# Comparison rows kept in a PSUM bank, and running counts of bins by a comparison and an addition in one VectorE operation

## The chip, the cores and the metric

The kernel runs on one core of a Trainium2 chip. The metric is the device time of one execution in microseconds (us). The core's engines are TensorE (PE in the profile, its weight loads PEld), VectorE (DVE), ScalarE (ACT), GpSimd (POOL) and SyncE (SP), which here only issues transfers. SBUF and PSUM are its memories of 128 partitions; PSUM has eight banks of 512 float32 values per partition, and matrix products are written there.

## The reference

A graph layer with 12,500 nodes of 128 features and 400,000 edges, sorted by `dst`. Cut to what is computed:

```python
h    = maximum(layernorm(x), 0) @ W_in2f.T               # 12500 x 128
Wij  = (smu(edge_attr_20 @ W_f1.T + b_f1) @ W_f2.T + b_f2) * edge_weight[:, None]
x_ij = h[dst] * Wij                                      # 400000 x 128
agg  = segment_sum(x_ij, src, num_segments=12500)
out  = x + smu(agg @ W_o1.T + b_o1) @ W_o2.T + b_o2
# smu(v) = ((1 + a) * v + (1 - a) * v * erf(mu * (1 - a) * v)) / 2, a = 0.01, mu = 2.5
```

`dst` is sorted, so the rows `h[dst]` of neighbouring edges lie close together. `src` is random, so the sum over `src` needs a sort.

## The kernel before

**Tiles.** 128 edges make a tile (3125 of them), four tiles a *group* (782; `GRP`), two groups a *super* (`SUP` tiles), and 59 supers (118 groups) an *epoch*; the seventh and last epoch has 37 supers (74 groups, the last one a single tile). Nodes are cut into 98 *bins* of 128 (`NB`); the bin of an edge is the upper part of `src` (`hi_b`), its place in the bin the lower part (`lo_b`).

**A group's way.** Its 512 edges run through PE as `pu` (line 478, first layer), GELU on ACT (`ge`, 486), `sm` on DVE (494), `pw` on PE (528). `ph` (509) picks the rows of h by a one-hot matrix `oh` (made once per super at line 386); ACT copies it to `hg` (517); DVE multiplies the two to `mt` (538). PE transposes `mt` to `pt` (548), ACT scales it by the edge's weight into the message buffer `ms` (558; six buffers), DVE writes the edge's `lo` as a 129th column (555), and POOL scatters the four tiles, 128 rows each, into a DRAM buffer of the epoch by four indirect transfers (561). An `ms` buffer is free again once its transfers have landed.

**Where a row goes.** Each bin has a region of `CAP` rows in the epoch's buffer (768 rows, 512 in the last epoch), and an edge takes the next free slot. `bins` (392 to 415) makes, per group, the one-hot `po` over bins (399: 128 partitions x 4 tiles x 98 bins) by comparing a row of bin numbers `irow_b` with `hi_b`, and the running count `co` of each partition over the tiles before (410 and 413: one addition of 98 float16 values per tile, each on the result of the one before). `count` (419 to 445) multiplies `co` by ones and `po` by a triangle with 32768 on its diagonal into the PSUM tile `pc` (426, 427; two banks in turn), so that the edge's own bin holds 32768 plus its slot; `read` (447) takes that out on ACT by a Relu with a sum (456), and `number` (459) makes the row index `ix` of slot and bin on DVE (465).

**Summing up.** While epoch k scatters, the rows of epoch k-1 are read back bin by bin (`fetch`, 575), 12 x 128 rows at a time. `choose` (586) makes their one-hot matrices `se` by comparing the row 0..127 in `irow` with the column of `lo` values (593: 128 x 1536 float32), and `add` (597) multiplies rows and `se` into `pg` (606) and adds that to `agg` (617, 619). This starts four groups into an epoch (`WAIT`) and is spread over the rest of it. The last epoch's sums, and the output layers (`half`, 320, and `rest`, 332), come after the last scatter. In the first epoch the other rows of h are made instead (`others`, 660: lines 178 to 212).

**Order.** Around all this the order on PE, DVE, ACT and SP is the program's own (`manual_schedule`). Within the loop over groups (678) a step does `turn` and `send` of group g, `number`, `weigh`, `gather`, `take` of g+1, half of the sums, `mix` of g+1, `hide`, `bend`, `count`, `read`, `smooth` of g+2, `bins` of g+3 and the other half of the sums. So DVE's order in a step is `ms` (555), `ix`, `mt`, `sm`, `oh` in every second step, `po`, the `co` chain, and `se` and `agg` wherever the sums call for them. POOL holds nothing but the scatters once the loop runs. Before the loop the same functions are called for groups 0 to 2 (lines 633 to 654).

PSUM is full: `pc` and `pg` have two banks each, `ph`, `pu`, `pw` and `pt` one.

Of the kernel before, what the change touches and what calls it, by code (L numbers as in the profile page):

```python
# [9 lines left out]
F32 = mybir.dt.float32  # L10
BF = mybir.dt.bfloat16
# [3 lines left out]
ALU = mybir.AluOpType  # L15
# [4 lines left out]
P = 128  # L20
# [9 lines left out]
GRP = 4  # L30
# [9 lines left out]
def gnn_kernel(  # L40
# [19 lines left out]
    nc = tc.nc  # L60
# [4 lines left out]
    NB = (N + P - 1) // P  # L65
    LASTB = N - (NB - 1) * P
    def chunks(total, step):
        return [(a, min(step, total - a)) for a in range(0, total, step)]
# [7 lines left out]
    for n in PARTS:  # L76
        n = min(n, left)
# [6 lines left out]
    CAP, ZMIN = [], []  # L84
    for a, n in eps_of:
# [9 lines left out]
    const = ctx.enter_context(tc.tile_pool(name="const", bufs=1))  # L95
# [17 lines left out]
    irow = const.tile([P, P], F32, name="irow")  # L113
    nc.gpsimd.iota(irow, pattern=[[1, P]], base=0, channel_multiplier=0,
                   allow_small_or_imprecise_dtypes=True)
    irow_b = const.tile([P, P], BF, name="irow_b")
    nc.vector.tensor_copy(irow_b, irow)

    tri = const.tile([P, P], F16, name="tri")
    lift = const.tile([P, P], F32, name="lift")  # L120
# [97 lines left out]
    with tc.tile_pool(name="prep", bufs=1) as prep, \  # L218
# [44 lines left out]
        for a, m in chunks(NT // P, GRP) + [(NT // P, 0)]:  # L263
# [8 lines left out]
            elif NT % P:  # L272
                m = NT % P
# [71 lines left out]
    with tc.tile_pool(name="ld", bufs=4) as ld, \  # L345
# [4 lines left out]
            tc.tile_pool(name="ps2", bufs=2, space=PSUM) as ps2, \  # L350
            tc.tile_pool(name="ps1", bufs=1, space=PSUM) as ps1, \
            tc.manual_schedule(engines={ET.PE, ET.DVE, ET.Activation, ET.SP}):
        NF = 4
        fbufs = []
        for i in range(NF):
            fb = ld.tile([P, SUP * P], F32, name=f"f{i}", bufs=1)
            nc.vector.memset(fb, 1.0)
            fbufs.append(fb)
        groups = [(t0 + a, g) for t0, nt in sups for a, g in chunks(nt, GRP)]
        NG = len(groups)  # L360
        PER = SUP // GRP
        epoch = [k for k, (a, n) in enumerate(eps_of) for _ in range(n)]
        first = {a * PER: k for k, (a, n) in enumerate(eps_of)}
        loaded, onehot, bins_of, slots, hidden, taken = {}, {}, {}, {}, {}, {}

        def load(s):
# [3 lines left out]
            e0, n = t0 * P, nt * P  # L370
            fb = fbufs[s % NF]
            nc.sync.dma_start(fb[0:R, :n], f_t[:, e0:e0 + n])
# [16 lines left out]
        last = {}  # L389
        begins = {}  # L390

        def bins(g):


            if g >= NG:
                return
            t, n = groups[g]
            po = cnt.tile([P, GRP, NB], F16, name="po")
            nc.vector.tensor_tensor(po[:, :n], irow_b[:, :NB].unsqueeze(1).to_broadcast([P, n, NB]),  # L399
                                    hi_b[:, t:t + n].unsqueeze(2).to_broadcast([P, n, NB]), op=ALU.is_equal)  # L400
            co = cnt.tile([P, GRP + 1, NB], F16, name="co")
            if g in first:
                k = first[g]
                nc.vector.memset(co[:, 0], 0.0)
                m = sum(groups[i][1] for i in range(g, min(g + eps_of[k][1] * PER, NG)))
                begins[k] = (t, cnt.tile([P, max(n for _, n in eps_of) * SUP], F32, name="hic", bufs=2))
                nc.vector.tensor_scalar(begins[k][1][:, :m], hi_b[:, t:t + m], float(CAP[k]), None, op0=ALU.mult)
            else:
                pl, cl, nl = last.pop(0)
                nc.vector.tensor_add(co[:, 0], cl[:, nl - 1], pl[:, nl - 1])  # L410
            more = g + 1 in first or g + 1 in (NG, BY)
            for j in range(1, n + more):
                nc.vector.tensor_add(co[:, j], co[:, j - 1], po[:, j - 1])  # L413
            last[0] = (po, co, n)
            bins_of[g] = (po, co)

        counts = {}
# [1 line left out]
        def count(g):  # L419

            if g >= NG:
                return
            n = groups[g][1]
            po, co = bins_of.pop(g)
            pc = ps2.tile([P, GRP, NB], F32, name="pc")
            nc.tensor.matmul(pc[:, :n], ones_h, co[:, :n], start=True, stop=False)  # L426
            nc.tensor.matmul(pc[:, :n], tri, po[:, :n], start=False, stop=True)  # L427
            counts[g] = pc
            if g + 1 == BY:
                pt = ps1.tile([P, GRP * P], F32, name="ph")[:, :NB]  # L430
                nc.tensor.matmul(pt, ones_h, co[:, n], start=True, stop=True)
                mm = cnt.tile([P, 2], F32, name="mm")
                nc.vector.tensor_reduce(mm[:, 0:1], pt[:, :NB - 1], op=ALU.max, axis=AX.X)
                nc.vector.tensor_scalar(bad[:, 3:4], mm[:, 0:1], float(ZMIN[0]), None, op0=ALU.is_gt)
            if g + 1 in first or g + 1 == NG:

                k = epoch[g // PER]
                pt = ps1.tile([P, GRP, P], F32, name="ph")[:, 0, :NB]
                nc.tensor.matmul(pt, ones_h, co[:, n], start=True, stop=True)
                mm = cnt.tile([P, 2], F32, name="mm")  # L440
                nc.vector.tensor_reduce(mm[:, 0:1], pt, op=ALU.max, axis=AX.X)
                nc.vector.tensor_reduce(mm[:, 1:2], pt[:, :NB - 1], op=ALU.min, axis=AX.X)
                i = 4 + 2 * k
                nc.vector.tensor_scalar(bad[:, i:i + 1], mm[:, 0:1], float(CAP[k]), None, op0=ALU.is_gt)
                nc.vector.tensor_scalar(bad[:, i + 1:i + 2], mm[:, 1:2], float(ZMIN[k]), None, op0=ALU.is_lt)
# [140 lines left out]
        def choose(k, c):  # L586

            b = c * SPAN[k]
            if b >= NB:
                return  # L590
            m = min(SPAN[k], NB - b) * Q[k]
            se = rowp.tile([P, ROWS, P], F32, name="se", bufs=2)
            nc.vector.tensor_tensor(se[:, :m], irow.unsqueeze(1).to_broadcast([P, m, P]),  # L593
                                    rows_in[c][:, :m, P:P + 1].to_broadcast([P, m, P]), op=ALU.is_equal)
            sel[c] = se

        def add(k, b, q):

            g = b % GRP
            c, i = b // SPAN[k], b % SPAN[k]  # L600
            if q == 0 and g == 0:
                pgs[0] = ps2.tile([P, GRP, P], F32, name="pg")
            if q == 0 and i == 0:
                choose(k, c + 1)
            o = i * Q[k] + q
            nc.tensor.matmul(pgs[0][:, g, :], rows_in[c][:, o, 0:P], sel[c][:, o, :], start=(q == 0),  # L606
                             stop=(q == Q[k] - 1))
            if q < Q[k] - 1:
                return
            if i == SPAN[k] - 1 or b == NB - 1:  # L610
                rows_in.pop(c), sel.pop(c)
                fetch(k, c + AHEAD)
            if g == GRP - 1 or b == NB - 1:
                dst = agg[:, (b - g) * P:(b + 1) * P]
                src = pgs[0][:, :g + 1].rearrange("p b n -> p (b n)")
                if k == 0:
                    nc.vector.tensor_copy(dst, src)
                else:
                    nc.vector.tensor_add(dst, dst, src)
# [18 lines left out]
        for g in range(3):  # L638
            bins(g)
        count(0)  # L640
        read(0)
        count(1)
        read(1)
        number(0)
# [33 lines left out]
        for g in range(NG):  # L678
            s = g // PER
            k = epoch[s]  # L680
# [22 lines left out]
            if k and i == WAIT - 2:  # L703
                choose(k - 1, 0)
# [14 lines left out]
            hide(g + 2)  # L719
            bend(g + 2)  # L720
            count(g + 2)
            read(g + 2)
            smooth(g + 2)
            if g % PER == 0:
                pick((g + 4) // PER)
            bins(g + 3)
            parts(k - 1, hi)
            step()
            assert k == 0 or next(h_steps, None) is None
        k = EPOCHS - 1  # L730
        begin(k)
        choose(k, 0)
        mids, ends = [], []
        units_in = {}
# [41 lines left out]
    with tc.If(flag > 0):  # L776
        with tc.tile_pool(name="gl", bufs=1) as gl, tc.tile_pool(name="gps", bufs=1, space=PSUM) as gps:
# [11 lines left out]
            with tc.For_i(0, NT, 1) as t:  # L789
# [26 lines left out]
                                               op1=ALU.mult, accum_out=dup)  # L816
# [87 lines left out]
```

## Time and profile before

| | |
|---|---|
| median of three runs | 4601.06 us (4593.67 to 4603.17) |
| the profiled execution | 4605.67 us, its span 4603.9 us |
| granted TensorE clock, mean | 0.949 |
| PE busy | 3824.8 us (83%) |
| POOL busy | 3355.9 us (73%) |
| DVE busy | 3181.2 us (69%) |
| ACT busy | 2809.9 us (61%) |
| first scatter's start, last one's start | 93.6 us, 4405.8 us |
| DMA | 808.84 MB, mean 176 GB/s |

A row of the list of groups reads: line, engine, operation, result<-operands, shapes, count, then the engine's busy time with them in us, the mean of one in ns, and behind the second bar the engine's idle time just before them with what ended most of it. A row of a line's own view has the durations as minimum/median/maximum in ns, and the first and last start in us. A row of the timeline has the start in us from the span's start, the duration in us, engine, line and operation, and in brackets the idle time before it with what ended it.

### The profile page before, as it was taken

The numbers are of one execution on the slowest core, as the hardware profiler recorded it, in microseconds if no ns is written. First come the engines' busy times: TensorE is split into PE (matmuls) and PEld (weight loads), VectorE is DVE, ScalarE is ACT, GpSimd is POOL, SyncE is SP. The second block draws the span as 40 slices with busy tenths as digits, with TensorE's granted clock in tenths as the row PEclk, the third lists the DMA queues.
The fourth block names the chain that finished last, engine by engine and source line by source line (L and its number), as shares of the span: only waits on it lengthen the run. The fifth ranks groups of instructions, "written<-read, shape, count | busy, mean of one in ns | idle before, by whom it ended". The sixth has DMA issues, their size and how long they took to land. (4 is left out here: it accounts for less than half of the span.)

```text
span 4603.9 us, 73307 instructions
## 1 busy us (share of the span) xinstructions
PE 3824.8 (83%) x18332; PEld 2340.7 (51%) x18596; DVE 3181.2 (69%) x8458; ACT 2809.9 (61%) x11054; POOL 3355.9 (73%) x3137
## 2 busy tenths in 40 slices
PE   4777787988879888879888878888798888799967
PEld 2334434555545555545555545555455555466656
DVE  5876676767667667757766767667576676687746
ACT  3776785666656666657666666666576666566500
POOL 1777777777777777777777777777777777777720
PEclk9999998999999999989999989999999999899978
DMA  6945565656646656646655556556465555466556
GB/s 187 212 139 169 157 167 173 193 174 184 181 131 214 190 175 183 181 145 206 190 180 172 168 171 199 172 179 186 125 209 173 169 172 166 138 197 183 164 179 175
DMA packets 457331, 808.84 MB, mean 176 GB/s; under 512 B 82228, under 2 KB 258630, under 8 KB 456512
## 3 DMA queue, kind: packets, MB, share of 16 engines
q1 hardware_dynamic: 328136, 573.65, 43.1%
q0 software_dynamic: 101504, 212.48, 14.2%
q10 hardware_dynamic: 27256, 17.94, 1.3%
q8 instruction: 147, 2.41, 0.2%
q14 instruction: 288, 2.36, 0.2%
HBM read 449.68 MB, written 354.07 MB: 175 GB/s over the span
## 5 line engine op out<-in xcount | busy, mean ns | idle before, releaser
L561 POOL DMA_INDIRECT buf<-ms,ix x3125 | 3349.1, 1072 | 1050.3 <-issue 268.7
L558 ACT ACTIVATE ms<-pt,w_sb 128x128 f32<-128x128 f32 x3125 | 903.2, 386 | 905.8 <-DMA buf<-ms,ix 699.8
L606 PEld LDWEIGHTS pg<-se,rw 128*128 128x128 f32 x7840 | 1087.1, 195 | 189.9 <-issue 51.7
L606 PE MATMUL pg<-se,rw 128*128 128x128 f32 x7840 | 1109.0, 278 | 35.7 <-DVE se L593 35.6
L456 ACT ACTIVATE jk<-pc,nbig 128x98 f32<-128x98 f32 x3125 | 1034.8, 361 | 12.3 <-PE pc L427 11.9
L548 PE MATMUL pt<-ident,mt 128*128 128x128 f32 x3125 | 512.8, 288 | 561.3 <-DVE mt L538 558.1
L528 PE MATMUL pw<-sm,w_f 128*128 128x512 f32 x1564 | 923.5, 674 | 27.1 <-DVE sm L494 21.6
L538 DVE SCALAR_TENSOR_TENSOR mt<-pw,b,hg 128x512 f32<-128x512 f32 x782 | 584.7, 748 | 514.6 <-ACT hg L517 511.3
L478 PE MATMUL pu<-f,w_f 128*128 128x512 f32 x1564 | 813.8, 602 | 2.6 <-DVE sm L494 2.5
L486 ACT ACTIVATE ge<-pu 128x512 f32<-128x512 f32 x782 | 472.9, 605 | 395.4 <-PE pu L478 360.2
L593 DVE TENSOR_TENSOR se<-irow,rw 128x1536 f32<-128x1536 f32 x327 | 572.6, 1751 | 193.0 <-DMA rw<-buf 159.5
L456 ACT ACTIVATION_READ_ACCUMULATOR jk<-pc,nbig 128x1 f32 x3125 | 705.0, 226 | 0.0
L548 PEld LDWEIGHTS pt<-ident,mt 128*128 128x128 f32 x3125 | 355.3, 145 | 668.5 <-DVE mt L538 664.1
L509 PE MATMUL ph<-oh,hw 128*128 128x512 bf16 (+1 forms) x2082 | 651.5, 396 | 16.1 <-issue 3.1
L494 DVE SCALAR_TENSOR_TENSOR sm<-pu,ge 128x512 f32<-128x512 f32 x782 | 535.6, 685 | 150.6 <-ACT ge L486 143.8
L517 ACT ACTIVATE hg<-ph 128x512 f32<-128x512 f32 x782 | 471.4, 603 | 210.2 <-PE ph L509 207.9
L413 DVE TENSOR_TENSOR co<-co,po 128x98 f16<-128x98 f16 x2351 | 503.7, 214 | 81.3
L509 PEld LDWEIGHTS <-hw 128*128 128x128 bf16 x2346 | 239.2, 102 | 585.9 <-issue 493.6
L399 DVE TENSOR_TENSOR po<-irow_b,hi_b 128x392 f16<-128x392 bf16 x782 | 436.8, 559 | 0.0
L555 DVE CAST ms<-lo_b 128x4 f32<-128x4 bf16 x782 | 150.6, 193 | 315.9 <-DMA buf<-ms,ix 312.8
L528 PEld LDWEIGHTS pw<-sm,w_f 128*128 128x128 f32 x1564 | 244.1, 196 | 165.7 <-DVE sm L494 163.1
L426 PE MATMUL pc<-co,ones_h 128*128 128x392 f16 x782 | 257.9, 330 | 13.3 <-DMA rbc<-rel_dram 12.8
(114 smaller groups left out, 1771.2 us busy)
## 6 DMA issues: line engine op xcount, KB each, us to landing
rw<-buf SPq DMA_DIRECT2D x326, 774.0 KB
buf<-zero SPq DMA_DIRECT2D x294, 387.0 KB
rbc<-rel_dram SPq DMA_DIRECT2D x390, 256.0 KB
buf<-ms,ix POOLq DMA_INDIRECT x3125
hw<-h_dram SPq DMA_DIRECT2D x391, 96.0 KB
f<-in_f_t SPq DMA_DIRECT2D x390, 80.0 KB
buf<-zero SPq DMA_DIRECT2D x49, 258.0 KB
h_dram<-hs SPq DMA_DIRECT2D x24, 384.0 KB
```

The costliest lines, as they stand in the source:

```text
L413: nc.vector.tensor_add(co[:, j], co[:, j - 1], po[:, j - 1])
L456: nc.scalar.activation(jk, pc[:, j], AF.Relu, bias=nbig, accum_out=sl[:, j:j + 1])
L478: nc.tensor.matmul(pu[:, :n], w_f1, loaded[g // PER][0][:, o:o + n], start=True, stop=True)
L494: nc.vector.scalar_tensor_tensor(sm[:, :n], units_of.pop(g)[:, :n], LIN, hidden[g][:, :n], op0=ALU.mult, op1=ALU.add)
L509: nc.tensor.matmul(ph[:, :n], hw[:, q * D:(q + 1) * D], oh[:, o:o + n], start=(q == 0), stop=(q == 2))
L528: nc.tensor.matmul(pw[:, :n], w_f2, hidden.pop(g)[:, :n], start=True, stop=True)
L538: nc.vector.scalar_tensor_tensor(mt[:, :n], pws.pop(g)[:, :n], b2, rows_of.pop(g)[:, :n], op0=ALU.add, op1=ALU.mult)
L548: nc.tensor.transpose(pt[:, j, :], mt[:, j * P:(j + 1) * P], ident)
L558: nc.scalar.activation(ms[:, j, 0:P], pt[:, j], AF.Copy, scale=w_sb[:, t + j:t + j + 1])
L561: i = nc.gpsimd.indirect_dma_start(out=bufs[k][:, :], out_offset=bass.IndirectOffsetOnAxis(ap=ix[:, j:j + 1], axis=0), in_=ms[:, j, :], in ...
L593: nc.vector.tensor_tensor(se[:, :m], irow.unsqueeze(1).to_broadcast([P, m, P]), rows_in[c][:, :m, P:P + 1].to_broadcast([P, m, P]), op=ALU ...
L606: nc.tensor.matmul(pgs[0][:, g, :], rows_in[c][:, o, 0:P], sel[c][:, o, :], start=(q == 0), stop=(q == Q[k] - 1))
```

## The change

One bank of PSUM (`rows_ps`) is filled once, ahead of the loop, with the row 0..127 (`irow_ps`) and, for each of the two values of `CAP`, with the row of bin numbers times `CAP` (`starts_of`). `po` and `se` compare with `irow_ps` in place of the SBUF rows `irow_b` and `irow`. The running count no longer reads `po`: each step compares the row of `starts_of` with the edge's bin times `CAP` (`hic`, which `number` used already) and adds the count of the tile before, in one scalar_tensor_tensor. The tile `pc` goes from two banks in turn to one, with its rows of 98 laid 128 columns apart. The bfloat16 copy `irow_b` goes.

```diff
-    irow_b = const.tile([P, P], BF, name="irow_b")
-    nc.vector.tensor_copy(irow_b, irow)
...
+        rows_ps = ps1.tile([P, GRP, P], F32, name="rows_ps")
+        irow_ps = rows_ps[:, 0]
+        nc.vector.tensor_copy(irow_ps, irow)
+        starts_of = {}
+        for c in CAP:
+            if c not in starts_of:
+                starts_of[c] = rows_ps[:, len(starts_of) + 1, 0:NB]
+                nc.vector.tensor_scalar(starts_of[c], irow[:, :NB], float(c), None, op0=ALU.mult)
...
-            t, n = groups[g]
+            (t, n), k = groups[g], epoch[g // PER]
             po = cnt.tile([P, GRP, NB], F16, name="po")
-            nc.vector.tensor_tensor(po[:, :n], irow_b[:, :NB].unsqueeze(1).to_broadcast([P, n, NB]),
+            nc.vector.tensor_tensor(po[:, :n], irow_ps[:, :NB].unsqueeze(1).to_broadcast([P, n, NB]),
                                     hi_b[:, t:t + n].unsqueeze(2).to_broadcast([P, n, NB]), op=ALU.is_equal)
...
-            else:
-                pl, cl, nl = last.pop(0)
-                nc.vector.tensor_add(co[:, 0], cl[:, nl - 1], pl[:, nl - 1])
+            t0, hic = begins[k]
             more = g + 1 in first or g + 1 in (NG, BY)
-            for j in range(1, n + more):
-                nc.vector.tensor_add(co[:, j], co[:, j - 1], po[:, j - 1])
-            last[0] = (po, co, n)
+            for j in range(g in first, n + more):
+                nc.vector.scalar_tensor_tensor(co[:, j], starts_of[CAP[k]], hic[:, t + j - t0 - 1:t + j - t0],
+                                               co[:, j - 1] if j else last.pop(0), op0=ALU.is_equal, op1=ALU.add)
+            last[0] = co[:, n - 1]
...
-            pc = ps2.tile([P, GRP, NB], F32, name="pc")
+            pc = ps1.tile([P, GRP, P], F32, name="pc")[:, :, 0:NB]
...
-            nc.vector.tensor_tensor(se[:, :m], irow.unsqueeze(1).to_broadcast([P, m, P]),
+            nc.vector.tensor_tensor(se[:, :m], irow_ps.unsqueeze(1).to_broadcast([P, m, P]),
                                     rows_in[c][:, :m, P:P + 1].to_broadcast([P, m, P]), op=ALU.is_equal)
```

More of the change, by code (lines that the diff above doesn't have):

```diff
@@ L402, in bins @@
             if g in first:
-                k = first[g]
                 nc.vector.memset(co[:, 0], 0.0)
```

## The prediction

> **What bounds the kernel now.** I read the page's list of groups first, then the scatter's own view (line 561), then a stretch of the timeline, and last the sums by stretch.
>
> ```profile
> L561 POOL DMA_INDIRECT buf<-ms,ix x3125 | 3349.1, 1072 | 1050.3 <-issue 268.7
> L558 ACT ACTIVATE ms<-pt,w_sb 128x128 f32<-128x128 f32 x3125 | 903.2, 386 | 905.8 <-DMA buf<-ms,ix 699.8
> ...
> L538 DVE SCALAR_TENSOR_TENSOR mt<-pw,b,hg 128x512 f32<-128x512 f32 x782 | 584.7, 748 | 514.6 <-ACT hg L517 511.3
> ...
> L593 DVE TENSOR_TENSOR se<-irow,rw 128x1536 f32<-128x1536 f32 x327 | 572.6, 1751 | 193.0 <-DMA rw<-buf 159.5
> ...
> L413 DVE TENSOR_TENSOR co<-co,po 128x98 f16<-128x98 f16 x2351 | 503.7, 214 | 81.3
> ...
> L399 DVE TENSOR_TENSOR po<-irow_b,hi_b 128x392 f16<-128x392 bf16 x782 | 436.8, 559 | 0.0
> ```
>
> PE shows the largest share (83%), but ACT spends 700 us waiting for message buffers (`ms`) that scatters have not given back. So the producers are held by the scatters. The view of line 561:
>
> ```profile
> L561 POOL DMA_INDIRECT buf<-ms,ix x3125: 956/962/2550, 93.6 to 4405.8; - x196
> ```
>
> From the first scatter's start at 93.6 to the last one's end at 4406.8 are 4313.2 us, of which 3349.1 are busy and 964.1 are gaps. The gaps are 0.30 us each, whatever is named as the releaser (3124 x 0.305 = 953): POOL really waits about 11 us in all. POOL is saturated. The median scatter takes 0.962 us, the mean 1.072, so 3349.1 - 3125 x 0.960 = 349 us are something extra that a scatter suffers. The timeline shows what:
>
> ```profile
> 2501.95 0.56 DVE L399 TENSOR_TENSOR po<-irow_b,hi_b 128x392 f16<-128x392 bf16 x1
> ...
> 2502.15 1.19 POOL L561 DMA_INDIRECT buf<-ms,ix  x1 [0.30 <-DMA buf<-ms,ix]
> ...
> 2504.12 1.76 DVE L593 TENSOR_TENSOR se<-irow,rw 128x1536 f32<-128x1536 f32 x1 [0.55 <-PE pg L606]
> ...
> 2504.90 1.80 POOL L561 DMA_INDIRECT buf<-ms,ix  x1 [0.30 <-DMA buf<-ms,ix]
> ...
> 2505.79 0.74 DVE L538 SCALAR_TENSOR_TENSOR mt<-pw,b,hg 128x512 f32<-128x512 f32 x1
> ```
>
> The scatter of 2504.90 ends at 2506.70, 0.82 after `se` ended (2505.88); that of 2502.15 ends at 3.34, 0.83 after `po` ended (2.51). It behaves as if it needs something 0.13 us after its start (0.96 - 0.83), which the DVE instruction holds to its end. `mt`, already running at 2505.88, did not hold it. I went through all 3125 scatters so: the extra of those over 0.975 us, given to the DVE instruction that ended 0.80 to 0.85 us before the scatter's end, is `se` 279.9 us (294 scatters), `po` 43.4 (169), `co` of line 410 6.9 (59), `co` of line 413 0.3 (12), `oh` 10.6 (82), `hs` of line 211 5.3 (13): 346.5 of the 349. And the other way round: the moment 0.13 us after the start fell inside `se` 307 times (294 held), inside `mt` 304 times (1 held), inside `agg` of line 619, an addition of an SBUF and a PSUM operand, 62 times (none held).
>
> **The change, part by part.**
>
> *Two SBUF operands become one SBUF and one PSUM operand (`se`, `po`, `co`).* The forms that come are those of `agg` (tensor_tensor) and `mt` (scalar_tensor_tensor with a column from SBUF), which held 0 of 62 and 1 of 304. POOL loses 279.9 + 43.4 + 6.9 + 0.3 = 330.5 us; `oh` and `hs` stay. [...]
>
> *The price of `se` and `po` on DVE.* The nearest rows are `agg` from PSUM at 681 ns and the addition of line 338 with both inputs in SBUF at 692, both 128x512: PSUM adds nothing. Both `se` (1.751 for 1536) and `po` (0.559 for 392) already run at about 1.04 ns per element plus 0.15, so they stay.
>
> *The price of `co`.* Four additions per group of 205 to 214 ns become four scalar_tensor_tensor on 98 elements with an SBUF column. Rows: the 128x98 `po` of the last tile, one element at a time, 249 ns; the 128x128 `mt` (with a column) 351 against the 128x128 `sm` (without) 280, so a column costs 71. Together 320 ns; ends 280 and 360. Each waits for the one before it (35 ns), as now. So 4 x 0.107 = 0.43 us per group, 335 us of DVE over the run; ends 0.27 and 0.6. On POOL's path it costs nothing while the producers keep ahead; whether they do is the main question, below. [...]
>
> *Do the producers keep ahead?* POOL alone needs per group 4 x (0.960 + 0.305) = 5.06 us, with what `oh` still holds 5.09; in epochs 1 to 5 it takes 5.53 now. The producers' own pace is read where they are not held: `mt` to `mt` in cycles in which ACT did not wait for `ms`, epochs 1 to 6: 4.08 us (27 cycles) without `se` and `oh`, 4.21 (29) with `oh`, 5.10 (20) with `se`, 5.65 (15) with both. `oh` comes in every second group, `se` in 49 of 118: 0.585 x 4.15 + 0.415 x 5.37 = 4.65. In cycles with `se` DVE is nearly full (4.6 to 5.0 of the 5.1 to 5.65), so these take the whole 0.43. In the others a loop over PE and ACT decides (`mt`, transposes, pw, ph, `hg`, `mt`: 0.75 + 0.58 + 0.96 + 0.85 + 0.61 and the hand-overs); DVE's own path, `mt` to `sm` 1.30, then `sm`, `po`, `co`, `ms`, `ix` 2.3, is 3.6 without and 4.0 with `oh`; with 0.43 more, 4.03 and 4.41, so 4.08 becomes 4.08 and 4.21 becomes 4.41, 4.25 in the mean. New pace 0.585 x 4.25 + 0.415 x 5.80 = 4.89, under POOL's 5.09. With 0.43 on every cycle it would be 5.08: a tie.
>
> *Where they don't.* In the last epoch `se` comes in 49 of its last 70 groups: 0.3 x 4.4 + 0.7 x 5.95 = 5.5 against 5.09, over 70 groups 29 us, less about 5 that are queued at its start: +24. In groups 60 to 90 of the first epoch, where the other rows of h are made, POOL already works at 5.45 to 6.03 per group and has its 11 us of real waits, so there is no gain there and up to 28 x 0.43 = 12 to lose: +8. At each epoch's start DVE waits for the first rows (159.5 us over 8 waits) and the queue at POOL falls from some 24 us to 5; it will refill by 0.2 us a group only, and two `se` close together can empty it: +15 for the five epochs, a guess between 0 and 40.
>
> *`pc` in one bank instead of two.* Its matmuls wait until ACT has read the group before. In the trace the first matmul of a group comes at least 1.95 us after that read's end (median 2.57), except for the second group (0.97 before): +1 us at the start, else nothing. Were a wait to come, the accumulations of line 606, then the next transposes and ACT's copies stand behind it. Its rows now lie 128 columns apart; no row shows such writes. I take nothing, as runs of 98 columns stay whole; as an upper end each takes its 330 ns again, 0.66 per group on a PE that issues its group in some 4.3 us when not held: 4.96, still under 5.09.
>
> *Start and end.* Two or three small writes to PSUM for one cast, and three groups of `co` ahead of the first scatter: 0.5 + 3 x 0.43, with the wait above +3 us. The 197.1 us behind the last scatter hold `se` at the same price; no scatter, no `co`: unchanged.
>
> **The sum**, for the profiled execution: 93.6 before the first scatter, 3349.1 busy, 964.1 gaps and 197.1 at the end are its span of 4603.9; it took 4605.7, and the runs' median is 4601.1, 4.6 lower. 4603.9 - 330.5 + 3 + 24 + 8 + 15 = 4323; as a run between 4320 and 4325: I say 4322.
>
> **The rivals.**
> 1. *The whole saving comes through*: DVE's extra time is absorbed everywhere; 4603.9 - 330.5 + 3 = 4276. For it: PE and DVE have idle time in the mean. Against: the cycles with `se`.
> [...]
> 3. *The new `co` hold POOL*, slower than before: one mechanism, at line 413's successor. 3126 instructions of 0.32 us are 1000 us of DVE; if they hold as `po` does (43.4 us of 437), POOL gains 100 us of waiting, if as `se` does (280 of 573) 490. It decides from 330 us on, 106 ns for each: at the `se` rate 4323 + 490 = 4810. Against: `mt`, the same kind of operands, 1 of 304.
> [...]
>
> **How the numbers follow.** A measurement can tell about 0.2% (9 us). Chances: the forecast 0.52 (own range 4290 to 4370), rival 1 0.16, rival 2 0.24, rival 3 0.05, rival 4 0.03. The low end 4265 is rival 1 with a little less from `oh`; the high end 4440 takes in rival 2's nearer half. Left out: its far half and rivals 3 and 4, under 0.2. Faster 0.92 (forecast, 1, 2), same 0.02 (half of 4), slower 0.06.
>
> **What would show it.** Right: mean scatter about 0.967 us with the median at 0.96, `se` at about 1.75 us, `co` at about 0.32, ACT's wait for `ms` down from 700 us to some 200 or less, POOL's real waits some tens of us, mostly in the last epoch. [...]

## The result

The changed kernel takes 4308.9 us (median of four runs, 4304.4 to 4310.2), the kernel before beside it 4602.1. The ratio is 0.9363 (95% interval 0.9347 to 0.9379). The profiled execution of the changed kernel has a span of 4308.4 us. Some of the experiments met two other chips, on which the kernel before takes 5334 and 5343 us; on the second of them the changed kernel ran too, and there it is 0.9% slower than the kernel before (last experiment).

The page's groups of the changed kernel (busy us, mean ns, then idle us before):

```profile
L566 POOL DMA_INDIRECT buf<-ms,ix x3125 | 3014.8, 965 | 1088.9 <-ACT ms L563 273.0
...
L563 ACT ACTIVATE ms<-pt,w_sb 128x128 f32<-128x128 f32 x3125 | 901.0, 387 | 388.4 <-PE pt L553 224.4
...
L417 DVE SCALAR_TENSOR_TENSOR co<-rows_ps,hic,co 128x98 f16<-128x98 f32 x3126 | 989.5, 317 | 83.2
...
L543 DVE SCALAR_TENSOR_TENSOR mt<-pw,b,hg 128x512 f32<-128x512 f32 x782 | 583.6, 746 | 234.8 <-ACT hg L522 231.1
...
L598 DVE TENSOR_TENSOR se<-rows_ps,rw 128x1536 f32<-128x1536 f32 x327 | 571.7, 1748 | 145.2 <-DMA rw<-buf 133.0
...
L406 DVE TENSOR_TENSOR po<-rows_ps,hi_b 128x392 f16<-128x392 f32 x782 | 433.6, 554 | 0.0
```

The mean scatter is at 965 ns, where 1072 were, and `se` and `po` cost what they cost before. The count operation takes 317 ns. ACT's wait for message buffers fell from 699.8 us to 145.9, and its largest releaser is now PE, so scatters and producers are close to balance:

```profile
ACT ms L563 <- DMA buf<-ms,ix: 145.9, 84, 20.9
```

The scatter's own view (minimum/median/maximum in ns, first and last start):

```profile
L566 POOL DMA_INDIRECT buf<-ms,ix x3125: 952/958/1440, 94.2 to 4110.0; - x196
```

The longest scatter fell from 2550 to 1440 ns. A stretch of the timeline has the case that the prediction showed, a scatter that starts inside `se`:

```profile
2706.69 1.75 DVE L598 TENSOR_TENSOR se<-rows_ps,rw 128x1536 f32<-128x1536 f32 x1
2707.36 0.96 POOL L566 DMA_INDIRECT buf<-ms,ix  x1 [0.30 <-issue]
```

It takes 0.96 us, where the one of 2504.90 took 1.80. Counted over all scatters, the moment 0.13 us after the start (the prediction's sign of a hold) fell inside `se` 399 times, inside `co` 702 and inside `po` 306 times, and in none of these did that instruction hold the scatter. Holds are left under `oh` (78 scatters, 11.7 us) and `hs` (20, 8.4 us).

Where the 295.5 us between the two spans went:

| | before | after | difference | forecast |
|---|---|---|---|---|
| up to the first scatter | 93.6 | 94.2 | +0.6 | +3 |
| scatters, busy | 3349.1 | 3014.8 | -334.3 | -330.5 |
| gaps between them | 964.0 | 1002.0 | +38.0 | +47 (8 + 24 + 15) |
| behind the last one | 197.1 | 197.4 | +0.3 | 0 |
| span | 4603.9 | 4308.4 | -295.5 | -280.5 |

The granted TensorE clock is 0.967 here and 0.949 before. The scatters alone account for more than the whole difference; whether the higher clock kept the gaps from growing further was not tested.

### The profile page after: what moved, and what is told of

The parts are those of the page before. It is cut to its first block, busy times and chain, and to the rows that moved or that the text cites. A ratio compares the mean times of both kernels' runs of the same rounds, so it can differ in the third digit from the quotient of the medians.

```text
span 4308.4 us, 74024 instructions
## 1 busy us (share of the span) xinstructions
PE 3746.9 (87%) x18332; PEld 2306.0 (54%) x18596; DVE 3473.9 (81%) x8460; ACT 2835.7 (66%) x11054; POOL 3021.5 (70%) x3137
## 5 line engine op out<-in xcount | busy, mean ns | idle before, releaser
L566 POOL DMA_INDIRECT buf<-ms,ix x3125 | 3014.8, 965 | 1088.9 <-ACT ms L563 273.0
L611 PEld LDWEIGHTS pg<-se,rw 128*128 128x128 f32 x7840 | 1074.4, 193 | 165.2 <-issue 21.7
L417 DVE SCALAR_TENSOR_TENSOR co<-rows_ps,hic,co 128x98 f16<-128x98 f32 x3126 | 989.5, 317 | 83.2
L533 PE MATMUL pw<-sm,w_f 128*128 128x512 f32 x1564 | 899.1, 657 | 26.0 <-DVE sm L499 20.3
L553 PE MATMUL pt<-ident,mt 128*128 128x128 f32 x3125 | 499.7, 283 | 357.7 <-DVE mt L543 355.8
L598 DVE TENSOR_TENSOR se<-rows_ps,rw 128x1536 f32<-128x1536 f32 x327 | 571.7, 1748 | 145.2 <-DMA rw<-buf 133.0
L461 ACT ACTIVATION_READ_ACCUMULATOR jk<-pc,nbig 128x1 f32 x3125 | 675.0, 216 | 0.0
L514 PE MATMUL ph<-oh,hw 128*128 128x512 bf16 (+1 forms) x2082 | 632.5, 386 | 15.0 <-issue 1.5
L406 DVE TENSOR_TENSOR po<-rows_ps,hi_b 128x392 f16<-128x392 f32 x782 | 433.6, 554 | 0.0
L483 PEld LDWEIGHTS pu<-f,w_f 128*128 128x128 f32 x1564 | 249.3, 193 | 23.2 <-DVE sm L499 4.1
```

The lines of the kernel that those rows point to most:

```text
L417: nc.vector.scalar_tensor_tensor(co[:, j], starts_of[CAP[k]], hic[:, t + j - t0 - 1:t + j - t0], co[:, j - 1] if j else last.pop(0), op0=A ...
L461: nc.scalar.activation(jk, pc[:, j], AF.Relu, bias=nbig, accum_out=sl[:, j:j + 1])
L483: nc.tensor.matmul(pu[:, :n], w_f1, loaded[g // PER][0][:, o:o + n], start=True, stop=True)
L514: nc.tensor.matmul(ph[:, :n], hw[:, q * D:(q + 1) * D], oh[:, o:o + n], start=(q == 0), stop=(q == 2))
L533: nc.tensor.matmul(pw[:, :n], w_f2, hidden.pop(g)[:, :n], start=True, stop=True)
L553: nc.tensor.transpose(pt[:, j, :], mt[:, j * P:(j + 1) * P], ident)
```

## The experiments

All of them give ratios to the kernel before, run on the same chip.

**Only `se` from PSUM.**

```diff
-            nc.vector.tensor_tensor(se[:, :m], irow.unsqueeze(1).to_broadcast([P, m, P]),
+            nc.vector.tensor_tensor(se[:, :m], irow_ps.unsqueeze(1).to_broadcast([P, m, P]),
```

(with the bank for `irow_ps`, and `pc` in one bank; all else as before)

> Of the change only se compares with the PSUM row (pc in one bank, po and the float16 counts as before). Theory, an instruction with two SBUF operands shuts a scatter out: the 280 us that se held go, the 43 of po and 7 of co stay, DVE does no more work than before, so no new waits: 4602 - 280 = 4322 us (4310 to 4335), mean scatter about 0.98 us. Rival, it was the counts no longer reading po, or the kind of instruction: about 4600 us with se still holding some 290 scatters.

Measured: 4343.5 us, ratio 0.9444 (0.9428 to 0.9459). From its page:

```profile
L564 POOL DMA_INDIRECT buf<-ms,ix x3125 | 3085.0, 987 | 1052.6 <-issue 283.0
...
L402 DVE TENSOR_TENSOR po<-irow_b,hi_b 128x392 f16<-128x392 bf16 x782 | 436.3, 558 | 0.0
```

No scatter is held by `se` any more (0 of 363), so it is the place of the operand that holds, not the kind of instruction: the rival falls. But the time lies outside the expected 4310 to 4335: `po` now holds 234 scatters for 58.7 us (before 169 and 43.4), and the first addition behind it 88 for 16.6 us (before 57 and 6.8). With `se` out of the way more of the scatters' moments land on what still holds (inside `po` some 330 in place of 276). Shares of a hold do not simply subtract.

**`se` and `po` from PSUM, the counts as before** (four float16 additions in SBUF).

```diff
-            nc.vector.tensor_tensor(po[:, :n], irow_b[:, :NB].unsqueeze(1).to_broadcast([P, n, NB]),
+            nc.vector.tensor_tensor(po[:, :n], irow_ps[:, :NB].unsqueeze(1).to_broadcast([P, n, NB]),
```

(on top of the one above)

> se and po compare with the PSUM row, the counts stay four float16 additions in SBUF. Theory as the trace of before reads (these additions hold next to nothing, 7 us): POOL loses 323 us, DVE nothing is added, so the 38 us of new waits of the changed kernel are not there either: 4602 - 323 = 4279 us (4272 to 4290), faster than the changed kernel. [...]

Measured: 4285.9 us (4284.4 to 4289.3), ratio 0.9321 (0.9305 to 0.9337), the shortest time of all, 23 us under the changed kernel.

```profile
L562 POOL DMA_INDIRECT buf<-ms,ix x3125 | 3015.6, 965 | 1066.4 <-issue 259.2
...
L414 DVE TENSOR_TENSOR co<-co,po 128x98 f16<-128x98 f16 x2351 | 501.9, 213 | 81.2
```

The scatters are as short as in the changed kernel (965 ns). The additions, two SBUF operands each, hold 95 scatters for 3.1 us together. The 6.8 us that line 410 held in the kernel before, and the 16.6 in the first experiment, were mostly `po` holding on into the addition behind it: with `po` in PSUM they are 2.0. So the new count operation wins POOL next to nothing and costs 0.1 us four times a group. POOL's real waits (what its gaps have beyond some 0.305 us each) are 27.9 us here and 49.5 in the changed kernel, and the difference of 21.6 is nearly all of the 23; of the 25.8 us between the two profiled spans, 4.1 more lie behind the last scatter. Some 12 of the 21.6 lie in groups 60 to 90, in which the other rows of h are made (real waits of 18.0 us against 30.2), and some 8 in the last epoch (6.8 against 15.0). The first shows in POOL's waits from 420 to 640 us, of the kernel before, of the changed one and of this experiment (us in total, times, longest; 0.3 us of each is the usual gap):

```profile
POOL buf L561 <- ACT hs L210: 15.5, 12, 1.9
...
POOL buf L566 <- ACT hs L208: 34.3, 15, 2.9
...
POOL buf L562 <- ACT hs L208: 23.1, 13, 2.5
```

The second shows in the last epoch, of the changed kernel (3680 to 4115 us) and of this experiment (3660 to 4095 us):

```profile
POOL buf L566 <- ACT jk L461: 34.7, 71, 1.5
...
POOL buf L562 <- ACT jk L457: 25.3, 66, 1.3
```

**Only the counts changed** (and `pc` in one bank; `se` and `po` compare with SBUF rows).

> Only the counts are the new operation with a PSUM row; se and po read SBUF rows as before. Theory: POOL keeps 323 to 340 of its 349 us extra and 5.5 us per group, the producers at 4.9 stay ahead in epochs 1 to 5, groups 60 to 90 lose some 15 us: 4600 to 4625 us. Rival, that DVE's 330 us of extra work are on the path in part: 4650 us or more. Rival, that the counts were what held: near 4310 us.

Measured: 4601.0 us, ratio 0.9997 (0.9985 to 1.0009).

```profile
L568 POOL DMA_INDIRECT buf<-ms,ix x3125 | 3333.4, 1067 | 1063.3 <-issue 257.6
...
L419 DVE SCALAR_TENSOR_TENSOR co<-rows_ps,hic,co 128x98 f16<-128x98 f32 x3126 | 992.2, 317 | 82.9
```

POOL keeps its holds (`se` 272.6, `po` 50.3 us), and 300 us more of DVE work (3482.3 busy against 3181.2) cost nothing that can be measured in the time, since POOL paces the whole; its real waits grow from 12.5 to some 24 us. Both rivals fall.

**Only `pc` in one bank, with its rows 128 columns apart.**

```diff
-            pc = ps2.tile([P, GRP, NB], F32, name="pc")
+            pc = ps1.tile([P, GRP, P], F32, name="pc")[:, :, 0:NB]
```

> The kernel before with pc in one bank and its rows of 98 laid 128 columns apart, nothing else. Theory: the first matmul of a group comes 1.95 us or more behind the read of the one before, so nothing changes: 4602 us within 9, matmuls of pc at 330 ns. Rival, the gaps in the rows or the bank cost something: matmuls of 400 ns or more, or ACT and PE waiting for each other at pc, visible as a time over 4611 us only if POOL runs dry.

Measured: 4609.7 us (4598.9 to 4617.6), ratio 1.0024 (1.0011 to 1.0036). The matmuls into `pc` stay at 330 ns, PE starts its next one 0.166 us (median) behind each of them in both traces, and POOL's real waits stay at 12.8 us (12.5 before), so gaps in the rows cost PE nothing and no wait arose. The 6 us between the profiled spans are 1.6 at the start, which is the second group's wait, 3.6 in scatters, of which `po` held 191 in place of 169, and 1.1 in gaps. Whether the 0.24% is a real cost or the way that scatters happen to meet `po` stays open; it is at most 0.36%.

**The rows of bin starts in SBUF**: the changed kernel, with two SBUF tensors in each count operation.

```diff
-                starts_of[c] = rows_ps[:, len(starts_of) + 1, 0:NB]
+                starts_of[c] = const.tile([P, NB], F32, name=f"starts{len(starts_of)}")
```

> The changed kernel, but the rows of bin starts lie in SBUF, so each of the 3126 count operations has two SBUF tensors (98 float32 and 98 float16) and takes about 0.32 us; po and se read PSUM. In the changed kernel the moment 0.13 us after a scatter's start fell inside a count operation 702 times. Theory A, an instruction shuts a scatter out for its whole length: 700 x 0.16 = 110 us more, 4420 us (4390 to 4440). Theory B, it shuts it out only while it reads (98 elements, about 0.1 of its 0.32 us), as the small holds of the float16 additions suggest (about 0.03 us each): some 230 held for 0.05 us, 12 us more, 4320 us (4312 to 4330). Theory C, only a plain comparison or addition of two tensors holds, not this kind of operation: 4309 us within 5, no scatter held by a co.

This ran on the first of the two slower chips: 5356.5 us, ratio 1.0038 (1.0001 to 1.0076) to the kernel before at 5333.5. Its time says nothing on the question, its scatters do: 94 of the 554 whose moment fell inside a count operation were held, 5.2 us together. On the second slower chip:

> The changed kernel with the rows of bin starts in SBUF, again. On the slower chip 94 of 554 moments inside a count operation were held, 0.055 us each, 5 us in all, which is theory B. On a chip like the first: the hold over the reading alone gives 7 to 12 us more than the changed kernel (ratio 0.938 to 0.941); over the whole operation 110 us (ratio 0.96).

5367.4 us, ratio 1.0060 (1.0026 to 1.0094), 88 of 559 held, 5.0 us. On the chip of the first four experiments:

> The changed kernel with the rows of bin starts in SBUF, a third try for a chip on which the kernel before takes 4601 us. Hold over the reading alone, as the slower chips showed (5 us in 94 and 88 scatters): ratio 0.937 to 0.941. On a chip where the kernel before takes 5340 us: ratio 1.005 again.

4309.1 us (two runs), ratio 0.9373 (0.9333 to 0.9413). 108 of 685 held, 5.9 us, median 0.053 us. A long hold among them is this one, in which a scatter's moment meets the third of four operations:

```profile
1172.45 1.38 DVE L417 SCALAR_TENSOR_TENSOR co<-starts,hic,co 128x98 f16<-128x98 f32 x4
1173.26 1.05 POOL L566 DMA_INDIRECT buf<-ms,ix  x1 [0.30 <-ACT ms L563]
```

Theory A, a hold over the whole operation, would have cost 110 us and falls; C, no hold at all, falls too; B stands, and even its 12 us were twice too many. For the counts it does not matter where the row of starts lies.

**`po` made twice**: the changed kernel with a second `po` in each group that nothing reads. DVE's busy time grows by 0.44 us per group (3815.8 against 3473.9 us), where 0.47 had been reckoned.

```diff
+            again = cnt.tile([P, GRP, NB], F16, name="again")
+            nc.vector.tensor_tensor(again[:, :n], irow_ps[:, :NB].unsqueeze(1).to_broadcast([P, n, NB]),
+                                    hi_b[:, t:t + n].unsqueeze(2).to_broadcast([P, n, NB]), op=ALU.is_equal)
```

> The changed kernel with po made a second time into a tile that nobody reads: 0.47 us more of VectorE in each group, from PSUM, so no hold on scatters. The prediction's reckoning of the producers' pace: 4.89 becomes some 5.3 us per group (cycles with se take all of it, the others most), over POOL's 5.07, so epochs 1 to 5 lose some 130 us, the last epoch 30, groups 60 to 90 some 14: 4480 us (4400 to 4530), with POOL waiting in all epochs. Rival, VectorE's work is hidden until its busy time per group (4.2 and 0.47) passes POOL's 5.07: 4340 to 4360 us, lost in groups 60 to 90 and the last epoch alone.

On the first slower chip: 5431.8 us, ratio 1.0180 (1.0096 to 1.0264). POOL really waits over 1100 us there, so the scatters are not the bound and the run tells nothing of the pace in question. On the second one:

> The changed kernel with po made a second time into a tile that nobody reads, again: 0.47 us more of VectorE per group. As before: by the prediction's reckoning of pace 5.3 us per group over POOL's 5.07, some 4480 us (4400 to 4530), POOL waiting in all epochs; rival, hidden until VectorE's busy time passes 5.07: 4340 to 4360 us.

5424.6 us, ratio 1.0177 (1.0109 to 1.0244), with the same waits. On the chip of the first four experiments:

> The changed kernel with po made a second time into a tile that nobody reads, a third try for a chip on which the kernel before takes 4601 us. There, by the prediction's reckoning of pace, 5.3 us per group over POOL's 5.07: 4480 us (4400 to 4530), ratio 0.957 to 0.985, POOL waiting in all epochs; rival, hidden until VectorE's busy time passes 5.07: ratio 0.943 to 0.948. On a chip where the kernel before takes 5340 us: ratio 1.018 again.

4356.9 us (two runs), ratio 0.9477 (0.9435 to 0.9518). That is the rival's 0.943 to 0.948 and not the 0.957 to 0.985 (4480 us) of the prediction's reckoning.

```profile
PE 3781.4 (87%) x18596; PEld 2306.0 (53%) x18596; DVE 3815.8 (88%) x9242; ACT 2861.4 (66%) x11054; POOL 3020.8 (69%) x3137
...
L569 POOL DMA_INDIRECT buf<-ms,ix x3125 | 3014.1, 965 | 1135.4 <-issue 289.8
```

DVE is at 88%, and POOL still runs at 5.07 to 5.11 us per group in epochs 1 to 5 (5.07 to 5.08 in the changed kernel). Its real waits grow from 49.5 to 95.1 us, and 74.7 of the 95.1 lie in groups 60 to 90 (43.2) and in the last epoch (31.5). Cycles (from one `mt` to the next) in which ACT was not held, groups 120 to 700, show what the reckoning missed: with `se` they went from 6.00 us in the changed kernel to 6.34, without it from 4.08 to 4.18. Of the 0.44 us, cycles with `se` took 0.34 and the others 0.10, in the mean 0.20: 5.07, just POOL's pace.

**The changed kernel and the second experiment, on the second slower chip.**

> The changed kernel once more, beside the kernel before on the same chip. In the last set of runs the kernel before took 5334 us, not 4601, with a granted clock of 0.89. If this chip runs as the first ones did: ratio 0.936 to the kernel before (0.93 to 0.945). If it runs as the last one did: the two runs there came out 0.4% and 1.8% slower than the kernel before, so the changed kernel is within 1% of it, as other things than the scatters bound the time.

> se and po from PSUM with the float16 counts, once more, for a comparison with the changed kernel on the same chip. If the chip runs as the first ones did: ratio 0.932 to the kernel before, some 0.5% under the changed kernel. Rival, the 23 us between them are a difference of chips: the same ratio within 0.2%.

Measured: the changed kernel 5380.9 us, ratio 1.0088 (1.0054 to 1.0123), so 0.9% slower than before; with the old counts 5297.1 us, ratio 0.9929 (0.9890 to 0.9969). The page of the changed kernel there:

```profile
PEclk8888888989888888888888988988998988999998
...
L566 POOL DMA_INDIRECT buf<-ms,ix x3125 | 3010.7, 963 | 2163.3 <-issue 821.1
```

The scatters are as short as on the first chip (963 ns), and none is held by `se` (0 of 197), but POOL really waits 1123 us for producers that are slower. The granted clock is 0.891 against 0.967. That cannot be all: `mt` to `mt` takes 6.06 us in the mean (314 cycles) even where the granted clock was full throughout, against 4.90 (569 cycles) on the first chip, and DVE and ACT sit idle in this trace without a releaser that it names. The idle time comes in long stretches: from 700 to 3600 us DVE waits over 3 us at a time 65 times there (303 us), and 5 times on the first chip (100 us). What makes the producers slow there stays open. What follows for the change: where producers bound the time, freeing POOL is worth little (46 us of the 323, with the old counts), and the longer counts are in part on the path: the two versions lie 84 us apart, against 23 on the first chip.

## Why the prediction was right

*POOL is the bound, and DVE's SBUF operands hold it.* Right: the first two experiments take the holds of `se` and of `po` away, one after the other, and the third leaves them and gains nothing. The forecast of 330.5 us against 334.3 measured is closer than its parts, by luck: the holds fell from 346.5 to 20.5 us, by 326, while `oh` and `hs` held 20.1 us where 15.9 had been counted on, and the scatters that nothing held were 3 ns shorter in the mean (958 for 961), some 9 us in all. That is not the change's doing: the median scatter is 958 ns with `pc` alone changed and 962 in the changed kernel with the bin starts in SBUF on the first slower chip.

*How long two SBUF operands hold.* The prediction took over what its trace had shown: the float16 additions hold next to nothing (0.3 us in 12 scatters for line 413). The trace was right: float16 additions hold 3 us when nothing holds ahead of them, and three traces with two SBUF tensors in the count show some 0.055 us for each one held, of an operation of 0.32.

*The price of `se`, `po` and `co`.* 1.751 became 1.748, 0.559 became 0.554, and `co` came to 317 ns where 320 was said (321 with its row in SBUF). The high end of 4440 and the chance of 0.24 for rival 2 count on an extra time for an operand in PSUM. No run shows one: the three came out 3 to 5 ns shorter with it.

*The producers' pace.* 4.89 was said; the same cycles of the changed kernel give 0.585 x 4.08 + 0.415 x 6.00 = 4.88. The parts were off in opposite ways: cycles with `se` came out at 6.00 (5.80 said), those without at 4.08 (4.25 said). That is luck in part, and `po` made twice shows it: there the same manner of reckoning gave 5.3 and the trace 5.07. With the old counts (second experiment) such cycles take some 5.4 and 4.2 us, as the prediction had read them from the kernel before (5.37 and 4.15), so the counts cost more than their own 0.43 us where `se` comes, and nothing where it does not.

*Where the producers don't keep ahead.* The sum of 47 us against 38 is right in size, but its terms are not, so that is luck too. Groups 60 to 90 gained 18.4 us of real waits (11.8 to 30.2; 8 was said): there the whole 0.43 us per group lies on the path (5.82 to 6.28 us per group), and some 4 us of the 18.4 are holds that became waits (these scatters' extra fell from 11.1 to 6.7 us). The last epoch gained 15.0 (24 said), at 5.26 us per group where 5.5 had been reckoned. That 5.5 used 4.4 and 5.95 us for the two kinds of cycle, for which the prediction gives no reason; its own 4.25 and 5.80 give 5.33, and +12. The guess of 15 us for the epochs' starts was wrong: epochs 1 to 5 gained 1.0 us together. The queue at POOL (from the end of ACT's write of a tile to the start of its scatter) does fall there, to 3.4 to 4.4 us, and has a median of 17.5 us in these epochs (25.0 before), so it hardly ever runs dry.

*`pc` in one bank*: nothing beside the 1 us at the start, as said, with the reservation of the fourth experiment.

*The rivals.* The whole saving (4276) is within 10 us of what the old counts reach (4285.9), but there because DVE has no extra work to absorb. The producers did not become the bound on the first chip and are it on the other two, in a way that the prediction had not named: not by DVE's price but as slower producers altogether, where the kernel before takes over 5300 us too. New counts that hold (0 of 702 scatters), and a hold by the kind of instruction (0 of 399 scatters in `se`), are excluded.

## What to carry to other kernels

When one engine's instructions are nearly all of one length and some are longer, ask which instruction of another engine ends a fixed time before each long one: that names the hold and its price by cause, before anything is changed. Move only the operands that hold: of the three in this change two gave all of the gain, and the third paid 0.1 us of VectorE work, four times a group, for nothing. And a gain on the bounding engine is worth what the next engine leaves of it, here a ratio of 0.936 on one chip and 1.009 on another, so measure it on more than one chip where the producers are only some per cent faster than it.

## What the runs showed of the hardware

A hold seems to last as long as the elements of an instruction take, not for the whole instruction. The time per element is read from the kernel before, where one `se` had 1024 elements per partition:

```profile
L593 DVE TENSOR_TENSOR se<-irow,rw 128x1536 f32<-128x1536 f32 x326 | 571.4, 1753 | 193.0 <-DMA rw<-buf 159.5 <-PE pg L606 33.2 <-issue 0.2
...
L593 DVE TENSOR_TENSOR se<-irow,rw 128x1024 f32<-128x1024 f32 x1 | 1.2, 1215 | 0.0
```

With 1751 ns, the median of the longer ones, that is 1.047 ns per element. In the same kernel the longest extra of a scatter behind `se` is 1.590 us, and 1536 elements take 1.608; behind `po` it is 0.412, and 392 elements take 0.410. Behind `oh` it is 0.257 (up to 0.28 in later traces) of an instruction of 0.491, and behind a float16 addition of line 413 0.039 of one of 0.214. That is 0.251 ns for each of 1024 elements and 0.40 ns for each of 98, both less than the 1.047 of `se`. What an element of these two takes was not tested; for `oh` the one instruction of 640 elements (0.379 us) beside the mean of 0.491 for 1024 gives some 0.29 ns, an estimate. The counts with two SBUF tensors fit: of 108 holds on the first chip all but two are at most 0.10 us, and 98 elements take 0.103; the other two, 0.11 and 0.14, came at the operation right behind `po`. The rest of an instruction, some 0.15 us of `se` and `po` (1.753 less 1.608, 0.559 less 0.410), leaves the scatter alone. So of the small instructions here with two SBUF operands most of the time does not hold (at most 0.044 of 0.21 us for the additions, some 0.055 of 0.32 for the counts).

A hold can run on into the next instruction: when `po` compared with an SBUF row, scatters were kept for up to 0.43 us (0.46 in the first experiment) until the first addition behind it ended, though that addition alone keeps one for 0.044 us at most (second experiment). Why it runs on is not shown.
